# Head-norm statistics of the first attention moved to PSUM, with a three-instruction Newton step

## The chip, the cores and the metric

The program runs on one core of a Trainium2 chip. A core has five engines that each work through their own list of instructions in order: PE (TensorE, matrix products), DVE (VectorE), ACT (ScalarE), POOL (GpSimd) and SP (SyncE, which here only issues DMAs). They meet through semaphores. Operands lie in SBUF (128 partitions) or in PSUM (128 partitions, eight banks of 512 fp32 values each). The metric is device time in microseconds (us), the median over runs of the whole program.

## The reference

A two-layer decoder over `x` of shape (4, 256, 256) and a context of shape (4, 256, 128); all fp32. Each layer adds an attention, a selective scan (Mamba) and a feed-forward part to `x`:

```python
x = x + L0_attn(layernorm(x)); x = x + L0_mamba(ctx, layernorm(x)); x = x + L0_ffn(layernorm(x))
x = x + L1_attn(layernorm(x)); x = x + L1_mamba(ctx, layernorm(x)); x = x + L1_moe(layernorm(x))
```

The change is in the first layer's attention. It has 8 query heads and 2 key/value heads of 32 values, rotates queries and keys, and then normalises every head of q, k and v by itself:

```python
def _layernorm_unit(x, eps=1e-06):
    mu = mean(x, axis=-1); xc = x - mu
    return xc * rsqrt(mean(xc * xc, axis=-1) + eps)
q = _layernorm_unit(q) * 256.0; k = _layernorm_unit(k); v = _layernorm_unit(v)
scores = mask64(q @ k.T / sqrt(32)); scores = tanh(scores / 30) * 30
out = softmax(scores) @ v
```

That is 12 heads (8 + 2 + 2) for each of 256 tokens, so with tokens on partitions in two chunks of 128 there are 24 means, 24 variances and 24 inverse roots on each partition for every batch element. The mixture of experts at the end (32 experts) takes the square root of its 128 gates per partition by the same helper.

## The kernel before

**Stages.** The first layer's attention runs per batch element b: `head0(b)` (L384 to L445) normalises x, projects to q, k and v, rotates, and normalises the heads; `tail0(b, ...)` (L456 to L551) transposes q and k, makes scores, tanh, exp, the weighted sum and the output projection, and adds to `x` (L551). Beside it runs the first layer's selective scan: 64 states of 128x512, each an exp on ACT (L238), a product on POOL (`db`, L240), a scan on DVE (L241) and a product on DVE (`hc`, L243); half of the `hc` are added up on PE (L258), half on POOL (L260). The feed-forward part of the first layer and the second layer follow. The code calls `head0(0)`, `head0(1)`, then in a loop over b: two scan steps (of two states each), `head0(b + 2)`, `tail0(b)`, in which two more pairs of scan steps stand.

**Order.** The Tile framework lays out each engine's list at build time with a planner of its own, from program order and planned durations. So a head's instructions come out between scan steps, and pieces from far down the program can come early. On the chip that order is then fixed: an instruction that waits holds up everything behind it on its engine.

**The head norms.** After the rotation DVE sums each head (`a_mean`, L417), centres it (L418), ACT squares (L422), DVE sums the squares (`a_rs`, L425), scales and adds epsilon (L426), and `rsqrt_steps` (L101 to L113) makes 1/sqrt: a start from the bit pattern (L105) and three Newton turns of four instructions (L109 to L112), all of 128x24 in SBUF tiles `rs_r` and `rs_t`. The root is multiplied into q by DVE (`qn`, L433), into v by DVE (`vn`, L436), and into k by POOL (`krep`, L440, two instructions).

**PSUM.** The eight banks of this stage are split into pools: `pa` (one bank: x transposed and the projections), `pb` (two banks: the transposes of q and k in `tail0`, then the score tiles, which it takes in pairs, and later the feed-forward products), `pc` (one), `psd` (two, the states), `psy` (one) and `pf` (one: convolution taps and the scan's front part).

**Same helper elsewhere.** `moe` (L975 on) calls `rsqrt_steps(gpos, 128)` twice, once for each half of the tokens, then multiplies root and gate (L987).

Of the kernel before, what the change touches and what calls it, by code (L numbers as in the profile page):

```python
# [10 lines left out]
F32 = mybir.dt.float32  # L11
# [3 lines left out]
ALU = mybir.AluOpType  # L15
AX = mybir.AxisListType

P = 128
# [23 lines left out]
def decoder_kernel(  # L42
# [27 lines left out]
    nc = tc.nc  # L70
# [3 lines left out]
    small = ctx.enter_context(tc.tile_pool(name="small", bufs=4))  # L74
    work = ctx.enter_context(tc.tile_pool(name="work", bufs=2))

    def ps(pool):
        return pool.tile([P, 512], F32, tag="ps", name="ps")

    def psum_pools(stack, **bufs):  # L80
        return [
            stack.enter_context(tc.tile_pool(name=n, bufs=k, space=bass.MemoryType.PSUM))
            for n, k in bufs.items()
        ]
# [13 lines left out]
    def load_x(b):  # L98
        nc.sync.dma_start(out=x[:, 2 * b : 2 * b + 2, :], in_=x_tok[:, 2 * b : 2 * b + 2, :])

    def rsqrt_steps(v, n):  # L101

        r_ = small.tile([P, n], F32, tag=f"rs_r{n}", name="rs_r")
        t_ = small.tile([P, n], F32, tag=f"rs_t{n}", name="rs_t")
        nc.vector.tensor_scalar(  # L105
            r_.bitcast(I32), v.bitcast(I32), -0.5, float(0x5F3759DF), ALU.mult, ALU.add
        )
        for _ in range(3):
            nc.vector.tensor_mul(t_, r_, r_)  # L109
            nc.vector.tensor_mul(t_, t_, v)  # L110
            nc.vector.tensor_scalar(t_, t_, -0.5, 1.5, ALU.mult, ALU.add)
            nc.vector.tensor_mul(r_, r_, t_)  # L112
        return r_  # L113


    def ln_stats(srcs):
# [14 lines left out]
    def ln_transposed(b, dst, pool):  # L131

        nb, rs = ln_stats([x[:, 2 * b + c, :] for c in range(2)])
        pt = ps(pool)
        for c in range(2):
            xn = work.tile([P, HID], F32, tag="xn", name="xn")
            nc.scalar.activation(
                xn, x[:, 2 * b + c, :], AF.Identity, bias=nb[:, c : c + 1], scale=rs[:, c : c + 1]
            )
            for f in range(2):  # L140
                nc.tensor.transpose(
                    pt[:, f * 256 + c * P : f * 256 + (c + 1) * P], xn[:, f * P : (f + 1) * P], ident
                )
        nc.scalar.copy(dst, pt.rearrange("p (f t) -> p f t", f=2))
# [181 lines left out]
    pa, pb, pc, psd, psy, pf = psum_pools(stage_a, pa=1, pb=2, pc=1, psd=2, psy=1, pf=1)  # L326
# [23 lines left out]
    with ExitStack() as ph:  # L350
# [30 lines left out]
            prs.append(wp.tile([P, 4, 384], F32, name=f"pr{k}"))  # L381
            nc.gpsimd.memset(prs[k][:, :, NEAR:256], E_LOW)

        def head0(b):  # L384
            xnT = work.tile([P, 2, S], F32, tag="xnT", name="xnT")
            ln_transposed(b, xnT, pa)

            r = ap.tile([P, 2, 12, 32], F32, tag="r", name="r")
            rr = ap.tile([P, 2, 10, 32], F32, tag="rr", name="rr")
            for c in range(2):  # L390
                pq = ps(pa)
                for f in range(2):
                    mm(
                        pq[:, 0:384],
                        lhsT=xnT[:, f, c * P : (c + 1) * P],
                        rhs=wqkv0[:, f, :],
                        start=(f == 0),
                        stop=(f == 1),
                    )
                cos = cst[:, C_COS0 + 32 * c : C_COS0 + 32 * c + 32]  # L400
                sin = cst[:, C_SIN0 + 32 * c : C_SIN0 + 32 * c + 32]
                q3 = pq[:, 0:320].rearrange("p (h d) -> p h d", d=32)
                nc.vector.tensor_mul(
                    rr[:, c].rearrange("p h (two d) -> p h two d", two=2),
                    pq[:, 0:320].rearrange("p (h two d) -> p h two d", two=2, d=16)[:, :, ::-1, :],
                    sin.rearrange("p (two d) -> p two d", two=2).unsqueeze(1).to_broadcast([P, 10, 2, 16]),
                )

                nc.vector.tensor_mul(q3, q3, cos.unsqueeze(1).to_broadcast([P, 10, 32]))
                nc.vector.tensor_add(r[:, c, 0:10, :], q3, rr[:, c])  # L410
                nc.scalar.copy(
                    r[:, c, 10:12, :], pq[:, 320:384].rearrange("p (h d) -> p h d", d=32)
                )

            rf = r.rearrange("p c h d -> p (c h) d")
            mean = small.tile([P, 24], F32, tag="a0_mean", name="a0_mean")
            nc.vector.tensor_reduce(mean, rf, AX.X, ALU.add)  # L417
            nc.vector.scalar_tensor_tensor(  # L418
                rf, mean.unsqueeze(2).to_broadcast([P, 24, 32]), -1.0 / 32, rf, ALU.mult, ALU.add
            )  # L420
            sq = ap.tile([P, 24, 32], F32, tag="sq", name="sq")
            nc.scalar.activation(sq, rf, AF.Square)  # L422
            rs = small.tile([P, 2, 12], F32, tag="a0_rs", name="a0_rs")
            rs24 = rs.rearrange("p c h -> p (c h)")
            nc.vector.tensor_reduce(rs24, sq, AX.X, ALU.add)  # L425
            nc.vector.tensor_scalar(rs24, rs24, 1.0 / 32, 1e-6, ALU.mult, ALU.add)  # L426
            rs = rsqrt_steps(rs24, 24).rearrange("p (c h) -> p c h", c=2)
            qn = ap.tile([P, 2, 8, 32], F32, tag="qn", name="qn")
            krep = ap.tile([P, 2, 2, 4, 32], F32, tag="krep", name="krep")

            vn = ap.tile([P, 2, 2, 33], F32, tag="vn", name="vn")
            nc.gpsimd.memset(vn[:, :, :, 32:33], 1.0)
            nc.vector.tensor_mul(  # L433
                qn, r[:, :, 0:8, :], rs[:, :, 0:8].unsqueeze(3).to_broadcast([P, 2, 8, 32])
            )
            nc.vector.tensor_mul(  # L436
                vn[:, :, :, 0:32], r[:, :, 10:12, :], rs[:, :, 10:12].unsqueeze(3).to_broadcast([P, 2, 2, 32])
            )
            for c in range(2):
                nc.gpsimd.tensor_mul(  # L440
                    krep[:, c],
                    r[:, c, 8:10, :].unsqueeze(2).to_broadcast([P, 2, 4, 32]),
                    rs[:, c, 8:10].unsqueeze(2).unsqueeze(3).to_broadcast([P, 2, 4, 32]),
                )
            return qn, krep, vn  # L445

# [109 lines left out]
        def states(n):  # L556

            while n > 0 and first:
                if next(first[0], "end") == "end":
                    s0.append(first.pop(0))  # L560
                else:
                    n -= 1

        s0 = []
        parts = [head0(0), head0(1)]
        for b in range(B):
            states(2)
            if b + 2 < B:
                parts.append(head0(b + 2))
            tail0(b, *parts[b], states)  # L570
            if b == 0:
                first.append(mamba_scan(mamba_front(0, 1, pf), [psd], psy))
            if b == 0:

                with tc.issue_after(loads[-1]):
                    nc.sync.dma_start(out=wqkv1, in_=wqkv1_in)
# [108 lines left out]
    with ExitStack() as ph:  # L685
# [289 lines left out]
        def moe(hf, ps_p, ps_h, acc):  # L975
# [8 lines left out]
            gpos = gp.tile([P, 4 * NE], F32, tag="gpos", name="gpos")  # L984
            nc.vector.tensor_scalar(gpos, gate.rearrange("p t e -> p (t e)"), 1e-30, None, ALU.max)
            root = rsqrt_steps(gpos, 4 * NE)
            done = nc.vector.tensor_mul(root, root, gate.rearrange("p t e -> p (t e)")).ins  # L987
            pg = ps(ps_p)
# [239 lines left out]
```

## Time and profile before

| what | value |
|---|---|
| median of three runs | 896.88 us (895.14 to 897.36) |
| profiled execution | 899.26 us, span of its instructions 897.5 us |
| busy in the span | PE 803.8, DVE 588.2, ACT 480.7, POOL 423.2 us |
| 30 to 135 us (heads, first two tails) | DVE 97.4 of 105, PE 90.3, POOL 64.8, ACT 58.0 |
| 135 to 190 us (last two tails) | DVE 44.7 of 55, PE 50.9, POOL 44.6, ACT 33.4 |
| 190 to 320 us (feed-forward of layer 0) | DVE 90.6 of 130, PE 110.1, POOL 89.1, ACT 93.4 |
| additions to `x` after the four tails (L551) | from 95.3 to 185.6 us |

Busy time is time in which an engine executes; the rest is waiting. An instruction's duration holds what it spends after it has started, also when it is held up by another engine inside its execution. So one form of instruction with widely different durations points to a resource that it shares. The chain that ended last is followed back from the end as far as 272 us; what bounds the time before that has to be read from the windows and the order of the instructions.

### The profile page before, as it was taken

What the parts mean: (1) busy time and instruction counts of PE and PEld (TensorE: products, weight loads), DVE (VectorE), ACT (ScalarE), POOL (GpSimd) and SP (SyncE); (2) the same over time, 40 slices, a digit from 0 to 9 for tenths busy, and PEclk for the clock granted to TensorE, in tenths of its full rate; (3) what the DMA queues carried; (4) which work ended last, traced back from release to release, by engine and by line L of the source; (5) the groups of instructions that cost most, each with busy time, mean ns of one, the idle gap of its engine ahead of it and who ended that gap; (6) DMA issues with size and microseconds to landing.
All of it is one profiled execution on the core that took longest, in us unless ns stands there. A gap on an engine that the chain in (4) does not pass through costs nothing.

```text
span 897.5 us, 10261 instructions
## 1 busy us (share of the span) xinstructions
PE 803.8 (90%) x3062; PEld 496.9 (55%) x3062; DVE 588.2 (66%) x1112; ACT 480.7 (54%) x1188; POOL 423.2 (47%) x427
## 2 busy tenths in 40 slices
PE   5788989978978989889898978997999999999997
PEld 2345656623433435546565745675666656666665
DVE  4897999775877668777759785788067676212121
ACT  5565545478848736746856693776333433211111
POOL 5654879865779624735635472422257751000000
PEclk9896889778986999999999999998999999999999
DMA  5545465672623400100110010000048743555542
GB/s 165 174 144 212 148 181 195 196 257 76 206 93 102 147 15 24 39 10 30 41 47 24 24 47 1 24 3 21 29 153 225 233 151 101 150 148 159 158 145 82
DMA packets 61015, 98.36 MB, mean 110 GB/s; under 512 B 6352, under 2 KB 26720, under 8 KB 60704
## 3 DMA queue, kind: packets, MB, share of 16 engines
q1 hardware_dynamic: 60080, 96.48, 34.4%
q10 hardware_dynamic: 880, 1.23, 0.4%
q8 instruction: 24, 0.39, 0.2%
q14 instruction: 31, 0.25, 0.1%
HBM read 96.24 MB, written 1.44 MB: 109 GB/s over the span
## 4 chain that ended last, share of the span: by engine, by line
PE 46%; DVE 12%; ACT 5%; POOL 3%; issue 3%; POOLq 0%; DVEq 0%; ACTq 0%
PE ps L1015 13%; PE ps L1029 12%; PE ps L883 5%; PE ps L714 4%; PE ps L868 2%; PE ps L821 2%; DVE ps L741 2%; DVE qs L734 1%; ACT sc L840 1%; DVE qr L742 1%; PE ps L748 1%; DVE h L241 1%; PE ps L669 1%; PE ps L643 1%; POOL sc L845 1%
## 5 line engine op out<-in xcount | busy, mean ns | idle before, releaser
L240 POOL TENSOR_TENSOR db<-bt,du 128x512 f32<-128x512 f32 x128 | 162.7, 1282 | 82.2 <-DVE h L241 57.0
L241 DVE TENSOR_TENSOR_SCAN h<-h,db 128x512 f32<-128x512 f32 x128 | 152.7, 1215 | 29.2 <-ACT h L238 28.1
L1015 PE MATMUL ps<-moe_xnT,w 128*128 128x512 f32 x272 | 128.9, 597 | 0.0
L1029 PE MATMUL ps<-w,hT 128*128 128x256 f32 x544 | 128.5, 379 | 0.0
L1020 DVE SCALAR_TENSOR_TENSOR hT<-ps,gr 128x512 f32<-128x512 f32 x64 | 44.1, 689 | 126.8 <-PE ps L1015 126.8
L238 ACT ACTIVATE h<-dt,negA 128x512 f32<-128x512 f32 x128 | 86.2, 689 | 73.5 <-DVE hc L243 71.2
L1029 PEld LDWEIGHTS ps<-w,hT 128*128 128x128 f32 x544 | 103.0, 190 | 40.2 <-issue 29.4
L1021 ACT ACTIVATE hT<-hT 128x512 f32<-128x512 f32 x68 | 42.8, 629 | 133.8 <-DVE hT L1020 133.6
L714 PE MATMUL ps<-wqkv,xnT 128*128 128x512 f32 x192 | 93.4, 598 | 8.0 <-DVE rq L706 5.6
L243 DVE TENSOR_TENSOR hc<-h,ct 128x512 f32<-128x512 f32 x128 | 84.8, 678 | 3.0 <-DMA ct<-bc 1.8
L250 POOL TENSOR_TENSOR y<-y,hc 128x512 f32<-128x512 f32 x64 | 80.8, 1272 | 8.3 <-DVE hc L243 6.4
L845 POOL TENSOR_TENSOR sc<-sc,rsum 128x512 f32<-128x512 f32 (+1 forms) x32 | 46.2, 1466 | 66.4 <-DVE rsum L843 66.3
L1015 PEld LDWEIGHTS ps<-moe_xnT,w 128*128 128x128 f32 x272 | 51.9, 192 | 36.5 <-issue 33.2
L707 POOL TENSOR_TENSOR rq<-rq,nhalf 128x8 f32<-128x8 f32 x20 | 33.0, 1651 | 80.9 <-DVE rq L706 80.7
L729 ACT ACTIVATE sq<-ps 128x128 f32<-128x128 f32 x160 | 42.4, 282 | 49.4 <-PE ps L714 49.4
L840 ACT ACTIVATE sc<-sc,nm 128x256 f32<-128x256 f32 (+1 forms) x128 | 56.7, 448 | 7.6 <-DVE nm L835 4.2
L883 PE MATMUL ps<-wo,oT 128*128 128x256 f32 x256 | 57.0, 381 | 0.0
L883 PEld LDWEIGHTS ps<-wo,oT 128*128 128x128 f32 x256 | 48.1, 190 | 8.9 <-ACT oT L876 2.6
L714 PEld LDWEIGHTS ps<-wqkv,xnT 128*128 128x128 f32 x192 | 32.7, 190 | 30.1 <-issue 17.5
L258 PE MATMUL ps<-hc,ident 128*128 128x512 f32 x64 | 39.9, 712 | 8.8 <-DVE hc L243 8.8
L260 POOL TENSOR_TENSOR y<-y,hc 128x512 f32<-128x512 f32 x32 | 40.8, 1274 | 4.8 <-DVE rs_t L110 2.1
L748 PE MATMUL ps<-ident,qr 128*128 128x128 f32 x160 | 28.1, 293 | 13.7 <-DVE qr L742 11.8
(206 smaller groups left out, 1450.6 us busy)
## 6 DMA issues: line engine op xcount, KB each, us to landing
bt<-bc SPq DMA_DIRECT2D x96, 256.0 KB, 3.5
ct<-bc SPq DMA_DIRECT2D x96, 256.0 KB, 3.8
w<-in_w_dram SPq DMA_DIRECT2D x64, 256.0 KB, 3.7
gr<-gt SPq DMA_DIRECT2D x64, 256.0 KB, 3.4
wqkv<-in_wqkv_dram SPq DMA_DIRECT2D x1, 3072.0 KB, 11.8
wo<-in_wo_dram SPq DMA_DIRECT2D x1, 2048.0 KB, 9.3
x<-in_x_dram SPq DMA_DIRECT2D x4, 256.0 KB, 5.1
w<-in_ws_dram SPq DMA_DIRECT2D x4, 256.0 KB, 3.9
```

The lines of the kernel that those rows point to most:

```text
L238: nc.scalar.activation(h, dt[:, c, :], AF.Exp, scale=negA[:, a : a + 1])
L240: nc.gpsimd.tensor_mul(db, bt, du[:, c, :])
L241: nc.vector.tensor_tensor_scan(h, h, db, 0.0, ALU.mult, ALU.add)
L243: nc.vector.tensor_mul(hc, h, ct)
L250: nc.gpsimd.tensor_add(y[:, c, :], y[:, c, :], state(n, c, bt, ct))
L714: mm(pq, lhsT=xnT[:, f, c * P : (c + 1) * P], rhs=wqkv1[:, f, ch * 512 : (ch + 1) * 512], start=(f == 0), stop=(f == 1),)
L840: nc.scalar.activation(part, part, AF.Exp, bias=nm[:, qc, j : j + 1], accum_out=rsum[:, qc, j : j + 1])
L845: nc.gpsimd.tensor_mul(part, part, rsum[:, qc, :].unsqueeze(2).to_broadcast([P, 4, w]))
L883: mm(pout[:, c * 256 : (c + 1) * 256], lhsT=oTs[h // 4][:, h % 4, c * P : (c + 1) * P], rhs=wo1[:, 8 * gp + h, :], start=(h == 0), stop=(h ...
L1015: mm(ph_, lhsT=w[:, f * P : (f + 1) * P], rhs=xnT[:, f, :], start=(f == 0), stop=(f == 1))
L1020: gated.append(nc.vector.scalar_tensor_tensor(h, ph_, 0.0, g, ALU.max, ALU.mult).ins)
L1029: mm(po[t // 2][:, (t % 2) * 256 : (t % 2 + 1) * 256], lhsT=h[:, t * P : (t + 1) * P], rhs=w[:, 256:512], start=start and t % 2 == 0, stop ...
```

## The change

The three small results (sums, variances with their roots, and the helper's scratch) are no longer SBUF tiles but three 24-column slices of one PSUM bank, taken from `pb` for the first two batch elements and from `pf` for the last two. The Newton turn is written with three instructions in place of four: t = v·r, t = (t·-0.5)·r, r = (t + 1.5)·r; the last turn writes its result over `v`, and the helper returns `v`. DVE's products for q and v read the root from PSUM. POOL's product for k reads a copy of it in SBUF (`rk`), which ACT makes. The helper's new form also serves the experts' gates, whose tiles stay in SBUF.

```diff
-    def rsqrt_steps(v, n):
+    def rsqrt_steps(v, n, room=None):
         r_ = small.tile([P, n], F32, tag=f"rs_r{n}", name="rs_r")
-        t_ = small.tile([P, n], F32, tag=f"rs_t{n}", name="rs_t")
+        t_ = room or small.tile([P, n], F32, tag=f"rs_t{n}", name="rs_t")
...
-        for _ in range(3):
-            nc.vector.tensor_mul(t_, r_, r_)
-            nc.vector.tensor_mul(t_, t_, v)
-            nc.vector.tensor_scalar(t_, t_, -0.5, 1.5, ALU.mult, ALU.add)
-            nc.vector.tensor_mul(r_, r_, t_)
-        return r_
+        for turn in range(3):
+            nc.vector.tensor_mul(t_, v, r_)
+            nc.vector.scalar_tensor_tensor(t_, t_, -0.5, r_, ALU.mult, ALU.mult)
+            to = v if turn == 2 else r_
+            nc.vector.scalar_tensor_tensor(to, t_, 1.5, r_, ALU.add, ALU.mult)
+        return v
...
-        def head0(b):
+        def head0(b, stats):
...
-            mean = small.tile([P, 24], F32, tag="a0_mean", name="a0_mean")
+            pn = ps(stats)
+            mean, rs24, room = [pn[:, 24 * k : 24 * k + 24] for k in range(3)]
...
-            rs = small.tile([P, 2, 12], F32, tag="a0_rs", name="a0_rs")
-            rs24 = rs.rearrange("p c h -> p (c h)")
...
-            rs = rsqrt_steps(rs24, 24).rearrange("p (c h) -> p c h", c=2)
+            rs = rsqrt_steps(rs24, 24, room).rearrange("p (c h) -> p c h", c=2)
+            rk = small.tile([P, 2, 12], F32, tag="a0_rs", name="a0_rs")
+            nc.scalar.copy(rk, rs)
...
-                    rs[:, c, 8:10].unsqueeze(2).unsqueeze(3).to_broadcast([P, 2, 4, 32]),
+                    rk[:, c, 8:10].unsqueeze(2).unsqueeze(3).to_broadcast([P, 2, 4, 32]),
...
-        parts = [head0(0), head0(1)]
+        parts = [head0(0, pb), head0(1, pb)]
...
-                parts.append(head0(b + 2))
+                parts.append(head0(b + 2, pf))
```

## The prediction

> **What bounds the kernel now.** I read the windows first, because the chain that ended last reaches back only to 272 us and all the head norms lie before 133. Columns: stretch, its length, then busy us (instructions) of PE, PEld, DVE, ACT, POOL, the clock, DMA share, GB/s.
>
> ```profile
> 30.00:135.00 105.00, 90.25 (x406) 55.67 (x404) 97.43 (x167) 57.99 (x117) 64.79 (x59) 0.83 0.51 166
> 135.00:190.00 55.00, 50.89 (x237) 30.98 (x235) 44.73 (x68) 33.39 (x63) 44.59 (x42) 0.88 0.65 194
> ```
>
> DVE is the tightest engine while the heads run (93% of 105 us), PE is next (86%), and after the heads PE leads (93% of 55 us). So DVE time saved here is worth something, but PE stands close behind.
>
> Second, the groups by form, DVE, 28 to 135 us. The last columns are busy us, mean ns, idle before.
>
> ```profile
> L241 DVE TENSOR_TENSOR_SCAN h<-h,db 128x512 f32<-128x512 f32 x28 | 33.8, 1217 | 1.0 <-POOL db L240 0.9
> L243 DVE TENSOR_TENSOR hc<-h,ct 128x512 f32<-128x512 f32 x26 | 17.4, 677 | 0.4 <-DMA ct<-bc 0.3
> ...
> L111 DVE TENSOR_SCALAR rs_t<-rs_t 128x24 f32<-128x24 f32 x12 | 5.7, 477 | 0.1
> L109 DVE TENSOR_TENSOR rs_t<-rs_r 128x24 f32<-128x24 f32 x12 | 4.8, 399 | 0.1
> L418 DVE SCALAR_TENSOR_TENSOR r<-a_mean,r 128x768 f32<-128x768 f32 x4 | 4.2, 1050 | 0.0
> L433 DVE TENSOR_TENSOR qn<-r,rs_r 128x512 f32<-128x512 f32 x4 | 3.8, 962 | 0.0
> ```
>
> A 128x24 instruction costs on average 0.40 or 0.48 us, nearly as much as the twenty times larger `hc`. Third, the order in time of DVE shows that this is no price of the operation:
>
> ```profile
> 119.89 0.17 DVE L112 TENSOR_TENSOR rs_r<-rs_r,rs_t 128x24 f32<-128x24 f32 x1
> ...
> 121.46 1.17 DVE L110 TENSOR_TENSOR rs_t<-rs_t,a_rs 128x24 f32<-128x24 f32 x1
> ...
> 123.15 0.70 DVE L111 TENSOR_SCALAR rs_t<-rs_t 128x24 f32<-128x24 f32 x1
> 123.77 0.41 DVE L450 TENSOR_TENSOR at<-ps,rden 128x256 f32<-128x256 f32 x1
> 124.10 0.98 DVE L112 TENSOR_TENSOR rs_r<-rs_r,rs_t 128x24 f32<-128x24 f32 x1
> ```
>
> One form takes 0.17 or 0.98 us. POOL runs a `db` or `y` product of 1.27 us through these moments, and the long ones end where POOL's does (POOL's `db` pair runs 120.11 to 122.59; the 1.17 ends at 122.63). Instructions with an operand in PSUM do not stretch: L450 here, `hc` (677 ns mean with `h` in PSUM), L410 (473 to 491 over eight). So these forms, with all operands in SBUF, are held while POOL works (the sums L417, L425 and the start L105 are not), and those that read one side from PSUM are not.
>
> **The change part by part.** All sums are made against the profiled run (899.26, span 897.5); the median is 2.38 lower, and I subtract the same gain from it.
>
> *The holds go.* Uncontended, the small forms take 0.17. The 56 of them (L109 to L112 x12 each, L105 and L426 x4 each) take 4.8 + 3.6 + 5.7 + 3.4 + 0.7 + 1.9 = 20.1 us; 56 x 0.17 = 9.5; so 10.6 us is hold. `qn` has a fastest of 0.64 and a mean of 0.96: 1.3 us over four. `vn` takes 0.70 each time, always beside `krep`, against 0.29 for a 128x128 product in the experts' stage: 1.6. L418 takes 1.05 against 0.95: 0.4. Together 13.9 us: 3.6 in head 0, 4.6 in head 1, 1.8 in head 2, 3.9 in head 3. Bounds: 0 (PSUM does not help) to 13.9; I take 13.9, because the PSUM rows above are nearest and none stretches.
>
> *Twelve instructions go* (one of four in three turns of four heads). Between independent neighbours a small one holds DVE for 0.10 (46.15 to 46.25), in an uninterrupted chain for 0.22 (80.78 to 80.99). 1.2 to 2.6; I take 1.2.
>
> *PSUM as the place.* L410 reads 320 columns from PSUM in 0.480 and `hc` 512 in 0.677, so 1.03 ns a column and 0.150 fixed; the SBUF form of 24 gives 0.166 - 0.025 = 0.141. 44 instructions at 9 ns more: 0.4 us. Upper bound from the reciprocal of 8 PSUM values, 0.198: 44 x 0.03 = 1.3. I take 0.5. [...]
>
> *The copy for POOL.* ACT gains four copies of 24 columns; the nearest row is L411 (64 columns) at 0.21, so 0.8 us on an engine busy 58 of 105. The dearer part is a new wait. Two engines that only read one bank are kept apart: L411 starts after L410 each time though their columns differ (46.25 + 0.48 against 46.81), and in the second layer:
>
> ```profile
> L734 DVEq EVENT_SEMAPHORE  x29: 21/21/1269, 318.3 to 611.7; - x29
> its engine sat idle before it (us, times) until:
>   ACT sq L729: 9.5, 7
> ```
>
> DVE's `qs` and ACT's `sq` both read the projection, and DVE waits. [...] `rk` stands before `qn` in the program, so `qn` and all behind it on DVE (scans, `hc`, and through them ACT's next exp) wait for the copy: 0.08 to start it, 0.21, 0.06 back, 0.35 a head, 1.4 in all. Upper bound: the copy stands behind an exp (0.69) and a table load (1.28), 2.3 a head, 9.3 in all; lower bound 0, where other DVE work lies between. I take 1.4, since L411's own gap is the nearest row. POOL's `krep` gets its root 0.35 later; PE's transposes wait for it, but before they came 2.7 after `krep` ended (52.4 to 55.06), which covers it.
>
> DVE relief: 13.9 + 1.2 - 0.5 - 1.4 = 13.2 us.
>
> *What arrives.* PE is next: I let its 90.25 us of work in this stretch go no denser than in the second window, 93%, which makes 97.0 of the 105. So 8.0 arrives, between 0 and 13.2. Beyond 190 us the stages start when the last tail has ended (186), so they shift with it.
>
> *The banks.* `pb` has two banks, which heads 0 and 1 now hold from the first sum to the last product. `tail0(0)` takes its score tiles from `pb` in pairs, so it needs head 1 to be through. Before, its scores began at 57.24, in the middle of head 1's Newton turns (58.50 to 70.73, `vn` until 72.5 + 0.7 = 73.2). Now head 1 ends at 73.2 - 3.6 - 4.6 - 0.6 (six instructions) + 0.7 (two copies) = 65.1, or about 59 if the planner also drops the six scan steps of 1 us that lay between. Without the hold the scores would have begun at 57.24 - 3.9 = 53.3. The slip is 6 to 12 us on PE's list. PE's idle 3.23 us at 75.61 and DVE's 4.12 at 87.85, both waits inside tail 0, take up part, and scans can be brought forward meanwhile: 9 - 3.2 - 4.1 = 1.7 lost; bounds 0 and 12. The `pf` bank of head 2 is asked for from 70.7 on, when the scan's front part has only its last two products left (80 and 90 us); their states are due after 101, so I cost it at nothing, or about 10 us of late states if they were due at once. Head 3 is alone in `pf`; the taps there are 10 us later.
>
> *The experts.* Two calls, three turns each: 2 x 0.33 + 0.27 + 0.33 = 1.26 a turn becomes 3 x 0.33 = 0.99, so 0.8 us a call. The chain runs through the first call (604.3 to 607.5), not through the second, where DVE waits for PE afterwards (3.65). 0.8, bounds 0 and 0.8.
>
> Sum: 8.0 - 1.7 + 0.8 = 7.1. Profiled run 892.2, median 896.9 - 7.1 = 889.8: **890**.
>
> **The rivals.** *Bank hold (slower).* The tail's slip of 12 us comes through undiminished, since PE is 91 to 100% busy from 50 to 70 and its work would pile up where it is just as busy later. For it: the score pair needs both banks. Against it: the 7.4 us of waits inside tail 0. 896.9 - 8.8 + 12 = 900.1; it ends slower from a net slip of 8.8 on.
>
> *DVE waits for ACT.* The copies stand behind exps and table loads: relief 13.2 - 7.9 = 5.3; through the same share (8.0 of 13.2) 3.2 arrives, less 1.7, plus 0.8: 894.6. For it: four table loads between 38 and 50. Against it: ACT is 45% idle.
>
> *PSUM does not end the holds.* If the cause were POOL's pace and not the operands' place, 1.2 - 0.5 - 1.4 leaves nothing, and it ends at 896 to 898. Against it: the PSUM rows.
>
> *Another order later.* The planner lays out everything after with shifted times; in the feed-forward part ACT alternates two tables, eight loads of 1.28 on the chain between 289 and 305. Eight more would be 10 us: 900.
>
> **How the numbers follow.** About 0.3% (2.7 us) is what a measurement can tell from no change: 894.2 to 899.6. Main case 0.54, 883 (13.2 + 0.8 arrive) to 894, all faster. Bank hold 0.20: slower 0.16, same 0.04. Wait for ACT 0.10: same 0.05, faster 0.03, slower 0.02. No end to the holds 0.06: same 0.05, slower 0.01. Another order 0.10: slower. Faster 0.57, same 0.14, slower 0.29. The range 883 to 902 leaves out some 0.16, mostly the worst of bank hold and order; the main case's own range is 883 to 894.
>
> **What would show it.** Right: L109 to L112's successors near 0.17 to 0.2 whatever POOL does, `vn` near 0.29, DVE near 84 us over the heads, the fourth L551 near 179 instead of 185.6, everything after shifted alike. Wrong: score products (L486) that start only after 60 with PE idle before; DVE idle before `qn` until an ACT copy; the fourth L551 early but the feed-forward part longer.

## The result, and the profile after

| | before | after |
|---|---|---|
| median | 897.1 us (895.14 to 897.36) | 912.38 us (900.86 to 914.54) |
| ratio, 95% interval | | 1.0138 [1.0093, 1.0183] |
| profiled execution, its span | 899.26, 897.5 | 912.61, 910.8 |
| mean granted TensorE clock in it | 0.941 | 0.927 |

The change made the kernel 1.4% slower; 890 was predicted. The changed program's executions differ more among themselves than those of the kernel before: 900.86 at a mean clock of 0.943, the other three 912 to 915 at 0.927 to 0.931. The run of 914.54 counts as a slow one (over 1.5% above the kernel's fastest); the mean of the other three is 1.3% above that of the kernel before. The spread is part of the answer.

**What the change was made for did happen.** The windows of the changed kernel, in the columns of those shown before:

```profile
30.00:135.00 105.00, 92.65 (x378) 55.48 (x377) 83.00 (x155) 56.25 (x119) 61.13 (x60) 0.77 0.46 150
135.00:190.00 55.00, 51.73 (x253) 34.58 (x251) 45.11 (x63) 28.32 (x57) 42.40 (x38) 0.91 0.70 215
```

VectorE fell from 97.43 to 83.00 us in the first stretch. TensorE did not get denser work from it: it is busy 2.4 us longer with fewer products (378 records for 406), at a clock of 0.77 for 0.83. The groups by form, VectorE, 28 to 135 us, show that the head norms are not held any more; the number after the busy time is the mean in ns:

```profile
L418 DVE TENSOR_REDUCE ps<-r 128x24 f32<-128x768 f32 x4 | 3.8, 950 | 0.0
...
L609 DVE TENSOR_SCALAR wmean<-wmean 128x10 f32<-128x10 f32 x4 | 3.3, 814 | 0.0
...
L434 DVE TENSOR_TENSOR qn<-r,ps 128x512 f32<-128x512 f32 x4 | 2.7, 680 | 1.0 <-ACT a_rs L428 1.0
L110 DVE SCALAR_TENSOR_TENSOR ps<-ps,rs_r 128x24 f32<-128x24 f32 x12 | 2.1, 175 | 0.0
...
L112 DVE SCALAR_TENSOR_TENSOR rs_r<-ps,rs_r 128x24 f32<-128x24 f32 x8 | 1.4, 170 | 0.0
...
L437 DVE TENSOR_TENSOR vn<-r,ps 128x128 f32<-128x128 f32 x4 | 1.1, 278 | 0.0
```

The steps take 170 to 175 ns where they averaged 284 to 477, and `vn` 278 where it took 697. (L609, a small step of a later stage that stays in SBUF, took 160 at each of its three places in this stretch before; it now stands beside GpSimd's products and takes 814.) The order in time of VectorE shows that the head norms' steps are even, whatever stands beside them, with one short wait for ScalarE's copy:

```profile
37.05 0.17 DVE L110 SCALAR_TENSOR_TENSOR ps<-ps,rs_r 128x24 f32<-128x24 f32 x1
37.73 0.17 DVE L112 SCALAR_TENSOR_TENSOR rs_r<-ps,rs_r 128x24 f32<-128x24 f32 x1
...
53.48 0.69 DVE L434 TENSOR_TENSOR qn<-r,ps 128x512 f32<-128x512 f32 x1 [0.96 <-ACT a_rs L428]
```

**Where the time was lost.** The additions to `x` that end the four tails, on VectorE's timeline, before:

```profile
95.29 0.69 DVE L551 TENSOR_TENSOR x<-x,ps 128x512 f32<-128x512 f32 x1
132.52 0.67 DVE L551 TENSOR_TENSOR x<-x,ps 128x512 f32<-128x512 f32 x1
157.48 0.68 DVE L551 TENSOR_TENSOR x<-x,ps 128x512 f32<-128x512 f32 x1
185.64 0.69 DVE L551 TENSOR_TENSOR x<-x,ps 128x512 f32<-128x512 f32 x1 [1.49 <-PE ps L543]
```

and after:

```profile
83.13 0.69 DVE L552 TENSOR_TENSOR x<-x,ps 128x512 f32<-128x512 f32 x1 [0.67 <-PE ps L544]
140.84 0.67 DVE L552 TENSOR_TENSOR x<-x,ps 128x512 f32<-128x512 f32 x1
163.72 0.68 DVE L552 TENSOR_TENSOR x<-x,ps 128x512 f32<-128x512 f32 x1
191.09 0.69 DVE L552 TENSOR_TENSOR x<-x,ps 128x512 f32<-128x512 f32 x1
```

The first tail ends 12 us earlier, the second 8 us later, the fourth 5.5 us later. The last feed-forward addition of the first layer comes at 328.27 for 316.76, and the last output addition at 906.21 for 892.86. So in this profile, of the 13.4 us, 5.5 are there when the last tail ends, 11.5 when the first layer ends, and little is added after it.

What moved is the front part of the second scan. Before, TensorE did its tap products (L189) at 29 to 46 us and its last products (L211) at 69.66 and 78.03:

```profile
29.14 2.07 PE L189 MATMUL ps<-ctxT,taps 128*128 128x512 f32 x2 [0.51 <-DVE taps L343]
...
78.03 2.07 PE L211 MATMUL ps<-xdbl,dtproj 8*128 8x512 f32 x2
```

Now they stand behind head 2's use of the `pf` bank, which ends with its `vn` at 78.27 to 78.54:

```profile
78.97 1.02 PE L189 MATMUL ps<-ctxT,taps 128*128 128x512 f32 x2
...
98.87 1.12 PE L211 MATMUL ps<-xdbl,dtproj 8*128 8x512 f32 x2
106.94 2.07 PE L211 MATMUL ps<-xdbl,dtproj 8*128 8x512 f32 x2
```

VectorE's order in time then has holes, the two largest of the stretch:

```profile
109.77 0.69 DVE L216 TENSOR_TENSOR du<-dt,u 128x512 f32<-128x512 f32 x1 [4.63 <-ACT dt L213]
...
118.35 0.21 DVE L450 RECIPROCAL rden<-ps 128x8 f32<-128x8 f32 x1 [6.02 <-PE ps L525]
```

First it waits for that front part, then for a product of the tail. These holes alone are not the loss. A second profile of the changed kernel (`after_again`, below: 894.1 us at a clock of 0.949, for 897.5 before) has both of them, and its fourth tail ends ahead of the 185.64 of the kernel before:

```profile
106.42 0.69 DVE L216 TENSOR_TENSOR du<-dt,u 128x512 f32<-128x512 f32 x1 [4.02 <-ACT dt L213]
...
115.00 0.21 DVE L450 RECIPROCAL rden<-ps 128x8 f32<-128x8 f32 x1 [6.03 <-PE ps L525]
...
184.03 0.68 DVE L552 TENSOR_TENSOR x<-x,ps 128x512 f32<-128x512 f32 x1
```

In the first profile TensorE runs at half clock beside the holes, from 102 to 132 us, for which the columns of these 3.2 us windows are the same as above:

```profile
102.20:105.40 3.20, 3.20 (x11) 2.32 (x11) 2.94 (x4) 1.91 (x5) 3.20 (x3) 0.50 0.01 3
...
111.80:115.00 3.20, 3.20 (x18) 3.20 (x16) 0.53 (x1) 3.20 (x7) 0.00 (x0) 0.50 0.02 5
115.00:118.20 3.20, 3.20 (x17) 3.20 (x17) 0.00 (x0) 0.99 (x2) 0.00 (x0) 0.50 0.00 0
```

### The profile page after: what moved, and what is told of

It is laid out like the page before. It is cut to its first block, busy times and chain, and to the rows that moved or that the text cites. A ratio compares the mean times of both kernels' runs of the same rounds, so it can differ in the third digit from the quotient of the medians.

```text
span 910.8 us, 10224 instructions
## 1 busy us (share of the span) xinstructions
PE 815.8 (90%) x3062; PEld 505.1 (55%) x3062; DVE 577.0 (63%) x1094; ACT 477.9 (52%) x1189; POOL 419.7 (46%) x427
## 4 chain that ended last, share of the span: by engine, by line
PE 47%; DVE 13%; ACT 5%; POOL 3%; issue 3%; DVEq 0%; ACTq 0%; POOLq 0%
PE ps L1016 12%; PE ps L1030 12%; PE ps L884 5%; PE ps L715 4%; PE ps L869 2%; DVE h L241 2%; DVE ps L742 2%; PE ps L822 1%; PE ps L644 1%; DVE qs L735 1%; DVE qr L743 1%; ACT sc L841 1%; PE ps L749 1%; PE ps L670 1%; DVE hc L243 1%
```

## The experiments

Three theories stood at first. *Bank theory*: `pf` is handed out in program order, so the front part waits for head 2, and that is the loss. *Clock theory*: the planner laid the whole program out anew, and a new order may meet more half clock. *Place theory*: PSUM operands or the copy cost more than they save.

### The bank hold alone, and the change without it

`e_hold` is the kernel before, with a bank of `pf` held by heads 2 and 3 from the sums to `vn`:

```diff
+            if b >= 2:
+                hold = ps(pf)
+                nc.vector.memset(hold[:, 0:1], 0.0)
...
+            if b >= 2:
+                held = small.tile([P, 1], F32, tag="held", name="held")
+                nc.vector.tensor_tensor(held, hold[:, 0:1], vn[:, 0, 0, 0:1], ALU.add)
```

> The kernel before with one thing added: heads 2 and 3 take the `pf` bank at their first sum (DVE writes one column of it) and give it up after `vn` (DVE reads that column). Statistics stay in SBUF, four instructions a turn. Bank theory (the loss comes from `pf` being given out in program order, so that the front part of the second scan queues behind head 2): its tap products (L189), which began at 29 us before, begin only after head 2's `vn`, 78 us or later, and the kernel takes 903 to 915. Clock theory (any newly laid order meets half-clock stretches of PE): no fixed direction, 890 to 912, following the mean granted clock. Place theory (PSUM operands or the copy to ACT cost the time): 896 to 899, since no statistic is in PSUM.

Measured: 907.22 us (906.79 to 908.49), ratio 1.0129 [1.0082, 1.0176]. The tap products begin at 87.75, as the bank theory had it, and a loss of the whole size appears with no statistic in PSUM, which the place theory did not allow. But this kernel is laid out anew too, so it does not part the hold from the new order.

`e_pa` is the changed kernel with heads 2 and 3 in a bank of `pa`:

```diff
-                parts.append(head0(b + 2, pf))
+                parts.append(head0(b + 2, pa))
```

> The changed kernel, but heads 2 and 3 take their statistics bank from `pa` (the bank of their own projections) in place of `pf`. Bank theory: the front part's tap products are back near 29 us, DVE keeps its relief of 14 us over 30 to 135, and the kernel takes 885 to 894. Clock theory: 900 to 912 again, with a clock near 0.93. Place theory: 905 to 912, since PSUM and the copy are still there.

Measured: 900.89 us (895.46 to 906.77, ten runs), ratio 1.0061 [1.0028, 1.0095]. The profile (of the fastest run, 895.46) has the tap products back at 28.72 us and the end of the fourth tail at 181.66, and half of the loss goes. Only half: the ratio stays above one, and the median above the bank theory's 885 to 894.

`e_first` keeps the PSUM form for heads 0 and 1 only; `e_sbuf` has no bank and no copy at all, only the three-instruction turn, 18 VectorE instructions fewer than before. In both, a head that is given `None` keeps its statistics in SBUF and makes no copy (that branch is not shown). Both calls below are those of `e_sbuf`; `e_first` changes the second only:

```diff
-        parts = [head0(0, pb), head0(1, pb)]
+        parts = [head0(0, None), head0(1, None)]
...
-                parts.append(head0(b + 2, pf))
+                parts.append(head0(b + 2, None))
```

> The changed kernel, but heads 2 and 3 keep sums, variances and Newton steps in SBUF (three instructions a turn, no copy); heads 0 and 1 have them in `pb` as in the change. Bank theory: tap products near 29 us, 8.2 of the 13.9 us of holds gone, 888 to 895. Clock theory: 897 to 912 with a clock below 0.935. Place theory: about half of the loss, 903 to 906.

Measured: 911.58 us (909.37 to 913.94), ratio 1.0184 [1.0125, 1.0243], at a clock of 0.931 to 0.937.

> The new three-instruction turn alone: all four heads keep everything in SBUF, no bank is held, no copy on ACT; the experts use the new turn too. Bank theory: tap products near 29 us, holds as before, 12 + 6 instructions fewer: 894 to 898. Clock theory: no fixed direction, 890 to 912. Place theory: 894 to 898 too.

Measured: 905.39 us (903.69 to 907.1), ratio 1.0106 [1.0058, 1.0155], at a clock of 0.940 to 0.945, that of the kernel before.

Both contradict the bank theory: `pf` is not held and the front part stands at its old place. `e_first` alone would agree with the clock theory. `e_sbuf` contradicts the place theory, and the clock theory too, since its clock is not lower. Fewer instructions, no bank and no copy to wait for, and 10 us slower: what was left was the order. (`e_frontfirst`, which writes the front part ahead of head 2 so that head 2 waits for `pf` instead, says the same.)

```diff
+            if b == 0:
+                front1 = mamba_front(0, 1, pf)
...
-                first.append(mamba_scan(mamba_front(0, 1, pf), [psd], psy))
+                first.append(mamba_scan(front1, [psd], psy))
```

> The changed kernel with one edit: the front part of the second scan is written ahead of head 2, so that it takes its bank of pf first and head 2 and head 3 wait for theirs instead. Bank theory (pf given out in program order makes the loss): 885 to 896, with the tap products back at their old place and the second tail's x add no later than 133. Order theory (every order laid anew is worse than that of the kernel before): 897 to 912. Place theory: 905 to 912.

Measured: 907.92 us (903.98 to 912.02), ratio 1.0142 [1.0075, 1.0209]. The tap products stand at 29.41 again and the second tail's addition at 133.77, but the kernel is as slow as the changed one.

### The instructions of one kernel in the order of the other

The order theory can be tried by itself. Each engine's list of the kernel before was written down, and edges of issue order alone (they make nothing wait for an end) hold another kernel's instructions to it (`ORDER`, the list, is not shown):

```diff
         decoder_kernel(tc, *args)
+        order = json.loads(zlib.decompress(base64.b85decode(ORDER)))
+        traced = list(nc.cur_bb.bb.instructions)
+        for chain in order:
+            for a, b in zip(chain, chain[1:]):
+                tc.add_manual_dep(
+                    traced[b],
+                    traced[a].name,
+                    mybir.DependencyInfo(
+                        mybir.DependencyClass.NoSync, mybir.DependencyReason.DATA
+                    ),
+                    reason="order",
+                )
```

`p_sbuf` is `e_sbuf` in the order of the kernel before, `p_border` the kernel before in the order of the changed one.

> The three-instruction turn, everything in SBUF, no bank and no copy (18 VectorE instructions fewer than before), with every instruction of every engine held to the order it has in the kernel before; the same instructions in an order laid anew took 905.4. Order theory (what was lost lies in the order in which the five engines' instructions stand, not in the instructions): 892 to 898, that is before less at most the 18 instructions. Instruction theory (the new turn costs time wherever it stands): 902 to 908. Clock theory (the clock meets each run at random and any kernel near here falls between 890 and 912): nothing nearer than 890 to 912, with a clock that explains the difference.

Measured: 893.57 us (889.87 to 895.57, ten runs), ratio 0.9966 [0.9939, 0.9993].

> The opposite: the instructions of the kernel before (four-instruction turn, SBUF, no bank, no copy) held to the order that they have in the changed kernel; the 18 VectorE instructions that the changed kernel lacks stand within their turns. Order theory: 908 to 920, the changed kernel's 912 and up to 8 for the old holds. Place theory (the bank, the products reading it and the copy cost the time, and the order only follows): 895 to 900. Clock theory: anywhere from 890 to 912.

Measured: 915.25 us (910.35 to 918.32), ratio 1.0222 [1.0166, 1.0279].

The same instructions take 905.4 or 893.6 us by their order alone, and the old instructions in the new order lose 2.2%. This settles where the loss is: in the order, not in the instructions, the bank as a place, or the copy.

### Which engine's order

`q_pe` and `q_dve` are `e_sbuf` with only TensorE's or only VectorE's list held (one chain in place of five).

> The three-instruction turn in SBUF as in the kernel that took 905.4 when its order was laid anew and 893.6 when every engine kept the order of the kernel before; here TensorE alone keeps that order and the other engines are laid anew. TensorE order theory (the loss lies in which products TensorE does first): 892 to 897. VectorE order theory (it lies in the order on VectorE): 901 to 908. Clock theory (no order matters as such): 890 to 912 with a clock that explains it.

Measured: 893.79 us (889.68 to 897.03, ten runs), ratio 0.9958 [0.9931, 0.9986].

> The same with VectorE alone held to its order of the kernel before and TensorE, ScalarE, GpSimd and the queues laid anew. TensorE order theory: 901 to 908. VectorE order theory: 892 to 897. If both this and the one with TensorE held come out at 897 or above, it takes the orders of both engines together.

Measured: 901.29 us (899.68 to 905.29), ratio 1.0065 [1.0037, 1.0092].

For the turn alone, holding TensorE's order recovers all of it, and holding VectorE's less than half. TensorE led in the second window before (93% of 55 us), so that fits, but the next three show that it can't be generalised. They hold the kernel before on TensorE alone: to the changed kernel's list (`q_after_pe`), to its own list with only the 14 products of the front part and its bank moved late (`q_front_late`), and the complement (`q_front_early`).

> The instructions of the kernel before, with TensorE alone held to the order that it has in the changed kernel; the other engines are laid anew around it. TensorE order theory: 908 to 918, near the 915.3 that all engines' orders gave. Other engines theory (VectorE or the queues carry it too): 897 to 906.

> The instructions of the kernel before, with TensorE held to its own order but for the products of the second scan's front part (8 tap products, 2 and 2 small projections, and the 2 products of later front parts that use the same bank), which stand where the changed kernel has them, behind head 2. Bank theory (this late front part is the loss): 906 to 918. Rest theory (the loss is in how scores, products of the weights and scan are interleaved): 895 to 902. Both parts: 902 to 908.

> The complement: the instructions of the kernel before, with TensorE held to the changed kernel's order but for the same 14 products, which stand where the kernel before has them. Bank theory: 894 to 900. Rest theory: 906 to 918. Both parts: 901 to 908.

Measured: 938.96 us (ratio 1.0478 [1.0436, 1.052]), 930.05 (1.0354 [1.0312, 1.0395]) and 931.26 (1.0378 [1.0326, 1.0431]). All three are far above every range given, and above the 915 that all five of the changed kernel's lists cost. The halves don't add up to the whole. One engine's list with the others laid anew around it is a third order, not a part of one. In `q_after_pe` VectorE's products `hc` wait 9.8 us for GpSimd's scan sums between 60 and 210 us, a wait that `p_border` doesn't have there. Which part of the changed kernel's order carries its loss stays open: holding the front part back on all engines together was not tried, since the states that follow from it would have had to move as well.

### How far an order laid anew can go either way

`e_one` is the kernel before with the three-instruction turn in head 0 alone, three instructions fewer:

```diff
-            rs = rsqrt_steps(rs24, 24).rearrange("p (c h) -> p c h", c=2)
+            rs = rsqrt_steps(rs24, 24, b == 0).rearrange("p (c h) -> p c h", c=2)
```

> The kernel before with the three-instruction turn in head 0 alone, in SBUF: three VectorE instructions of 0.2 us fewer, and an order laid anew. Order theory (the order of the kernel before is a good one, and any edit that re-lays it loses): 898 to 910. Instruction theory and place theory: 894 to 897, less than 1 us from before. Clock theory: 890 to 912.

Measured: 898.4 us (894.91 to 903.8, ten runs), ratio 1.004 [1.0011, 1.0069]. That is the lower edge of the order theory's range, and above the 894 to 897 of the other two: three short instructions fewer, and no gain.

In the order of the kernel before, head 0 can have a bank of `pb` and head 3 one of `pa`; heads 1 and 2 find none free for as long as they need it. `p_two` makes the change at those two heads, with the short turn at all, in that order; `f_two` is the same laid anew.

```diff
-        parts = [head0(0, pb), head0(1, pb)]
+        parts = [head0(0, pb), head0(1, None)]
...
-                parts.append(head0(b + 2, pf))
+                parts.append(head0(b + 2, (None, pa)[b]))
```

> The change at two of the four heads (head 0 with its sums in a bank of pb, head 3 in one of pa, both with the copy for GpSimd), the three-instruction turn at all, and the order of the kernel before on every engine; heads 1 and 2 stay in SBUF since that order leaves them no bank. Order theory: 888 to 894, the 893.6 of the same order without a bank and up to 5 less for the holds of heads 0 and 3 (3.6 and 3.9 us on VectorE). Place theory (bank and copy cost time): 896 to 902.

Measured: 890.41 us (887.57 to 894.41, nine runs), ratio 0.993 [0.9904, 0.9956]: the fastest of all kernels run here, 0.7% below the kernel before.

> The change at heads 0 (a bank of pb) and 3 (the bank of pa), the three-instruction turn at all, with no order held: the same instructions as in the run that took 890.4 in the order of the kernel before. Order theory (an order laid anew costs some 5 to 15 us whatever is in it): 896 to 908. Instruction theory (banks that leave the rest free are the whole matter): 888 to 893.

Measured: 896.02 us (891.41 to 901.07, ten runs), ratio 0.9974 [0.9944, 1.0005]. The order theory had put it at 896 to 908, so it holds at its very edge: a new order isn't always bad, and this one gave back over half of the gain rather than all.

`p_two` has both forms side by side, which makes it the cleanest view of the hold. From its groups by form, VectorE, 28 to 135 us (two heads each):

```profile
L113 DVE SCALAR_TENSOR_TENSOR rs_t<-rs_t,rs_r 128x24 f32<-128x24 f32 x6 | 3.1, 512 | 0.1
L112 DVE TENSOR_TENSOR rs_t<-a_rs,rs_r 128x24 f32<-128x24 f32 x6 | 3.0, 496 | 0.1
...
L113 DVE SCALAR_TENSOR_TENSOR ps<-ps,rs_r 128x24 f32<-128x24 f32 x6 | 1.1, 176 | 0.0
L112 DVE TENSOR_TENSOR ps<-ps,rs_r 128x24 f32<-128x24 f32 x6 | 1.0, 172 | 0.0
```

The same instruction, the same run: 496 to 512 ns from SBUF, 172 to 176 with one side in PSUM.

And its last tail ends 7.5 us earlier than in the kernel before, 13 us earlier than in the changed one:

```profile
178.18 0.69 DVE L562 TENSOR_TENSOR x<-x,ps 128x512 f32<-128x512 f32 x1 [1.49 <-PE ps L554]
```

### The changed kernel once more, and its clock

> The changed kernel once more, beside the kernel before on the same chip. Order theory: 904 to 914, that is a ratio of 1.010 to 1.018, and below the 1.022 of the old instructions in the same order by what the change itself is worth (4 to 8 us). Clock theory: the ratio moves with the mean clock, and a run whose clock equals that of the kernel before takes no longer than it.

Measured: 909.57 us (895.9 to 920.81, four runs), ratio 1.0124 [1.0048, 1.02]. The four runs are 895.9 at a clock of 0.949, 906.22 at 0.936, 912.92 at 0.929 and 920.81 at 0.924. The two with the higher clock have a mean 0.4% above that of the kernel before beside them, the other two 2.1%. Both forecasts hold: the median lies in the order theory's range, and the run at 0.949 takes no longer than the kernel before (897.3). This is one program, with one order and one set of instructions. The last lines of the view of cores, for the changed kernel's first profile and this one:

```profile
core 0: 910.8 us, clock 0.927
```

```profile
core 0: 894.1 us, clock 0.949
```

Span times clock is 844.3 in the first and 848.5 in the second: 16.7 us of difference in the time, and none of it in the work. This makes a sum possible that keeps the clock apart, the span counted at full clock, as a mean over the runs of each kernel:

| kernel | runs | mean clock | span x clock, us | median, us |
|---|---|---|---|---|
| before (beside these experiments) | 72 | 0.944 | 844.5 | 896.6 |
| after (both sets) | 8 | 0.934 | 847.5 | 912.4 |
| `p_border`: old instructions, new order | 4 | 0.932 | 850.4 | 915.3 |
| `e_hold`: the hold alone | 4 | 0.932 | 844.0 | 907.2 |
| `e_sbuf`: short turn, laid anew | 4 | 0.943 | 852.1 | 905.4 |
| `p_sbuf`: short turn, old order | 10 | 0.948 | 844.9 | 893.6 |
| `p_two`: two heads, old order | 9 | 0.946 | 841.2 | 890.4 |

An order can lose in two ways. `e_sbuf` loses 7.6 us of full clock, with the clock unchanged: TensorE stands idle longer (102.9 us of its profile for 93.7 before). `e_hold` loses nothing there, and all that it loses by a clock of 0.932. The changed kernel loses mostly by the clock: at that of the kernel before, 847.5 / 0.944 would be a span of 898, 3 us above the 895 that the same sum gives for the kernel before, and the other 10 or so of the 12.9 us between the mean times come with the clock. Its first profile says the same: TensorE is idle for 95.0 us, little more than the 93.7 before, but busy for 815.8 in place of 803.8 with the same 3062 products. So the clock theory holds for the changed kernel as an account of where the time is, and not for the short turn laid anew. The clock goes with the order, in the mean: 0.932 to 0.935 for the changed kernel, `p_border`, `e_hold`, `e_first` and `e_frontfirst`, 0.942 to 0.948 for the kernel before and all others, except the three that hold TensorE alone to a moved list (0.917 to 0.929). What in an order lowers it is not shown. That a low clock is a cause, and not the trace of a slower order, is supported only by runs of one program: in the changed kernel's own, where the order is the same, the time follows the clock.

## Why the prediction was wrong, by its own steps

*The holds go (13.9 us), PSUM as the place (0.5), the copy (1.4).* Right in mechanism and size. The rows of the head norms by form (28 to 135 us, without the sums) fall from 30.9 to 15.2 us, 15.7 less, for 14.6 predicted (13.9 + 1.2 - 0.5). That VectorE stands at 83.00 over 30 to 135, where about 84 was forecast, is partly luck: that stretch also has three scans and two `hc` fewer, and the longer L609. In `p_two` the steps in PSUM take 171 to 179 ns and the last ones of a turn, which no hold met in SBUF, 169 to 174, so the place costs at most 10 ns a step, as the 9 of the prediction had it. The wait for the copy is 0.96 us, at one head of four.

*What holds them.* The rows of `p_two` show which are held and by how much: the two forms above take 496 to 512 ns with all operands in SBUF and 172 to 176 with one side in PSUM, and the scaling with epsilon, which has one input, 472 and 179. All operands in SBUF do not always mean a hold: the last step of a turn takes 169 to 174 there. The sums take 929 to 954 ns in either place. By what way GpSimd's work holds an instruction of VectorE no run here shows.

*What arrives (8.0 of 13.2).* Near, where the order stays. `p_two` takes 9.4 us off VectorE's busy time over the whole span (588.2 to 578.8) and the median falls by 6.7. But `p_sbuf`, with no bank, has 2.4 of that already for 2.0 of busy time, so the two banks by themselves give some 3 to 4 us for 7.4. In the changed kernel's own order the change may be worth as much: its ratios of 1.0138 and 1.0124 lie 0.8 to 1.0% under the 1.0222 of the old instructions there, 7 to 9 us, though the intervals overlap, so that this is not shown (of span times clock it is 2.9 us, the rest is clock). The predicted net gain was 7.1. But the step took the old order for granted.

*The banks (1.7 lost, bounds 0 and 12).* Wrong on both. The `pb` hold was to delay the scores of tail 0; they begin at 47.54 instead of 57.24, and the first tail ends 12 us early. The `pf` bank ("so I cost it at nothing, or about 10 us of late states") sent the tap products 50 us later, and the hold with nothing else, laid out anew, takes 1.3% longer (`e_hold`). (The front part's last two products, put at 80 and 90 us there, begin at 69.66 and 78.03 in the trace.) The fourth tail was to end near 179; it ends at 191.09 (at 184.03 in the second profile), and at 178.18 in `p_two`. The step's error was to ask what the chip would wait for in the old order. None of the tap products shows a wait in the trace after: they stand later in the list, and the rest of the list around them is another.

*Another order later (0.10, 900 us).* This rival came true, at a greater price and in another place. It looked for the damage in eight more table loads of ScalarE in the feed-forward part; between 190 and 345 us there are 34 before and 34 after. The front part moved instead, holes opened on VectorE, and TensorE's mean clock fell from 0.944 to 0.934; the prediction had no term for the clock. With both sets of runs the order's price is the 2.2% of `p_border`, about 20 us, against the 10 that the rival named.

**The step that failed** is therefore the assumption under "What arrives" and "The banks", that the change would take effect in the order of the kernel before, with "Another order later" as the only place for a doubt about it. In its place the runs show that the new order alone, with the old instructions, takes 915.25 us (`p_border`), and the changed kernel 912.38. Given the old order, two of the four heads reach 890.41; that this is the number predicted for all four is chance.

*The other rivals.* Bank hold: a slower result, but not by the tail's scores. Wait for ACT and no end to the holds: excluded by the rows above. The 0.8 us of the experts were not tried apart.

## What to carry to other kernels

Where a planner lays out the lists, an edit is two changes: what its instructions cost, and a new order for everything. Hold the old order to price the first, and give the new instructions the old order if it proves better; a buffer that is handed out in program order is part of the order, even when no instruction ever seems to wait for it. And where TensorE leads, read span times clock beside the span, or a change of the clock will be taken for one of the work (here 844.3 and 848.5 for spans of 910.8 and 894.1 us).

## What the hardware showed that was not expected

The TensorE clock of one and the same program on one core varies between 0.924 and 0.949 from run to run, and its time between 920.8 and 895.9 us; the kernel before, over its 72 runs on four chips, varies between 0.936 and 0.954 (902.3 and 890.9). The half-clock stretches are partly tied to the program: in both profiles of the changed kernel one begins at 100 to 102 us, but it lasts until 132 in the first and 124 in the second, and those at 177 to 187 and 320 to 327 are in the first only.

A busy TensorE did not get the full clock back there, as far as the profile's modelled ends of products can be trusted: in the windows shown above TensorE is busy without a gap for 6.4 us from 111.8 on, and the clock stays at 0.50 until 132; in the same profile it is busy for the whole 10 us from 177 to 187, at 0.50. What keeps it there no run here shows.
